# A four-layer image network on one core: the scan rounds of eight images as one sequence, the second layer begun three rounds later, a sigmoid made from tanh

## The chip, the cores and the metric

The kernel runs on one core of one Trainium2 chip, as one launch. The metric is the device time of that launch in microseconds (us), lower is better. The core has five engines that [...] wait for each other through semaphores: PE (matrix products; PEld is its weight load), DVE (element-wise work and scans), ACT (activation functions), POOL (element-wise work; it also issues DMAs) and SP (issues DMAs only). [...]

## What is computed

The input x has 8 images of 384 channels and 32 x 32 pixels, all in float32. Four layers follow each other.

- Layer 0 is a selective state-space scan over the 1024 pixels of an image, forwards and backwards, beside a local branch. For each image the input is normalised over channels, projected to u and z, u is convolved with 4 taps, and from it come a step size delta and the rows B and C (16 states each). Then, for each channel and each of the 16 states,

```python
deltaA = jnp.exp(delta[..., None] * A)
deltaBu = (delta * u)[..., None] * Bm[:, :, None, :]

def step(h, inp):
    dA, dBu, c = inp
    h = dA * h + dBu
    return (h, jnp.einsum('bdn,bn->bd', h, c))
```

  The sum over states, plus u * D, is multiplied by silu(z) and projected out. The local branch is a depthwise 3 x 3 convolution whose sigmoid gates the normalised input; both are added to x with two learned scales.
- Layer 1 is a convolution block, a linear attention over 8 heads and an MLP of 384 to 1536 to 384 with gelu, each with a residual.
- Layers 2 and 3 are depthwise convolutions with large kernels, a pointwise convolution and a gelu. The change does not touch them.

## The kernel before, in words

Layers 0 and 1 are written in `_layers01`, image by image, and the two layers of different images are interleaved by hand. Three Python generators hold the work of one image; each `yield` ends one step and names its cost in units of about one 128x128 by 128x512 product.

- `front(b)` (from L572) is layer 0 ahead of the scan: normalisation (`ms`, L581 to L586), in-projection (`in`, `uz`, L592 to L605), local branch (`lc`, `lg`, `xr`, L608 to L623), 4-tap convolution (`ut`, `uc`, L626 to L646), B and C (`xd`, `bc_d`, L648 to L660), step sizes (`dt`, `sp`, `dl`, L662 to L693). Its steps cost 96 units in all. What DVE has to do after ACT is put off by `defer(1, ...)` to a later round: `local` (L617) for the gate, `deltas` (L680) for the step sizes. Results go to DRAM scratch: `dl_d`, `v_d`, `bc_d`, `ud_d`, `z_d`, `x1_d`.
- `scan(b)` (from L695) is the scan: 12 units (2 directions, 2 halves of 512 pixels, 3 channel groups of 128) of 4 rounds, so 48 rounds an image. The forward direction takes half 0 and then half 1, the backward direction half 1 and then half 0. A round handles 4 of the 16 states of 128 channels, as two tiles of 128 x 1024. For each tile ACT makes `da` with four exponentials a round (L776), DVE makes `du` (L781, in PSUM) and runs two scans into `hs` (L793), POOL multiplies by C (L802), and PE sums over states into `acc` (`sums`, L736). The sums are written two rounds late (the list `late`, L785 and L806), so that PE need not wait for POOL. After the fourth round of a unit `acc` goes out: forwards to `yf_d` (L746), backwards times z to `g_d` (L749, L750). The loads of a unit (`dlt`, `vr`, L728, from `dl_d` and `v_d`) are issued on SP one unit ahead, half of them in round 1 of the unit before (L767) and half in its last round (L811); the rows B and C (`bct`, L714) likewise (L788, L809). Only within an image: unit 0 of an image loads everything when the generator starts (L752, L753).
- `layer1(b)` (from L877) is layer 1: out-projection (`op`, `xx`, L881 to L891, which needs `g_d` and `x1_d`), first convolution (`h`, `dw`, L892 to L909), second (`c`, L910 to L923), attention (`kv`, `q`, `den`, `rzb`, `pj`, L927 to L1032), layer norm (`mu`, `var`, L1034 to L1051) and MLP (`mf`, `hm`, `mo`, L1053 to L1085). Its steps cost 328 units.

Two short generators fill in: `fold()` prepares layer-1 weights beside image 0, `kernels` (called `prepare`) the convolution kernels of layers 2 and 3 beside images 1 to 7.

The order of instructions is set in the loop at L1092: while the rounds of `scan(b)` are written, `front(b+1)` and `layer1(b-1)` are written between them. All their work is one sum `need` (90 + 325 + 12 units in the middle images), spread over 47 rounds; the generator that is least far on goes next:

```python
while work and done < need * (i + 1) / (rounds - 1):
    w = min(work, key=lambda w: w[2] / w[1])
```

When the 48 rounds of an image are written, the remaining sums are flushed (L815), then what is left of the two generators, then all that was put off (L1117 to L1120). Only then does the generator of the next image begin, with its loads. ACT and DVE serve scan and layers alike, in the order written: an `op` result that DVE has to add (L890) stands ahead of the scans of the next round. After image 7, `layer1(7)` runs by itself.

Of the kernel before, what the change touches and what calls it, by code (L numbers as in the profile page):

```python
# [1 line left out]

# [6 lines left out]
FP = mybir.dt.float32  # L9
AF = mybir.ActivationFunctionType  # L10
# [4 lines left out]
P = 128  # L15
# [359 lines left out]
def _layers01(tc, nc, B, xv, x2_d, dram, ident, mean_w, eps5, eps6, one, half, minus1, vec, bns, bnt,  # L375
# [12 lines left out]
    with ExitStack() as ctx:  # L388
# [183 lines left out]
        def front(b):  # L572
# [36 lines left out]
            for h in range(2):  # L609
                for c in range(NC):  # L610
                    xr = t2(f"xr_{b}_{h}_{c}")
                    nc.sync.dma_start(xr, xv[b][:, c, bass.ts(h, HALF)])
                    ps = conv3(xn_d, b % 2, h, c, t3, f"lc_{b}_{h}_{c}")
                    lc = t2(f"lg_{b}_{c}_{h}")
                    nc.scalar.activation(lc, ps, AF.Sigmoid, bias=vec("dw_b0", c))

                    def local(h=h, c=c, lc=lc, xr=xr):  # L617
                        nc.vector.tensor_mul(rows(lc), rows(lc), xn[h][c])
                        nc.vector.scalar_tensor_tensor(xr, lc, rs, xr, ALU.mult, ALU.add)
                        nc.gpsimd.dma_start(x1v[b][:, c, bass.ts(h, HALF)], xr)  # L620

                    defer(1, local)
                    yield 3  # L623
# [68 lines left out]
                    defer(1, deltas)  # L692
                    yield 3  # L693

        def scan(b):  # L695

            units = [
                (d, h, c)
                for d in range(2) for h in ((0, 1) if d == 0 else (1, 0)) for c in range(NC)
            ]  # L700
            late = []
# [2 lines left out]
                return t.rearrange("p (j n) -> p j n", n=HALF)  # L704

            def load_bc(k, r):
                d, h, _ = units[k]
                t = sp.tile([P, 2, HALF], FP, tag="bct", name=f"bct_{b}_{d}_{h}_{r}", bufs=4)
                for o in range(2):
                    src = bass.AP(  # L710
                        bc_d.tensor, bc_d[b, d, o * NST + 4 * r, h * HALF].offset,
                        [[0, 32], [L, 4], [1, HALF]],
                    )
                    nc.sync.dma_start(t[:, o, :], src)  # L714
                return t

            def load(k, i):

                d, h, c = units[k]
# [12 lines left out]
            def sums(k, r, hs, acc, y0, zt):  # L732
                d, h, c = units[k]
                cols = bass.ts(h, HALF)
                for j in range(4):
                    nc.tensor.matmul(  # L736
                        acc[32 * j : 32 * j + 32, :], selt, hs[j // 2][:, bass.ts(j % 2, HALF)],
                        start=(r == 0), stop=(r == NR - 1), skip_group_check=True,
                    )
                if r == 0:  # L740
                    nc.tensor.matmul(acc, ident, y0, start=False, stop=False, skip_group_check=True)
# [13 lines left out]
            for k, (d, h, c) in enumerate(units):  # L755
                cols = bass.ts(h, HALF)
                second = k % (2 * NC) >= NC
                for r in range(NR):
# [11 lines left out]
                    end = HALF - 1 if d == 0 else 0  # L770
                    for i in range(2):
                        dlt, vt = now[i]
                        da = sp.tile([P, 2 * HALF], FP, tag="da", name=f"da_{b}_{k}_{r}_{i}", bufs=N_DA)
# [6 lines left out]
                        du = accp.tile([P, 2 * HALF], FP, tag="du", name=f"du_{b}_{k}_{r}_{i}")  # L780
# [8 lines left out]
                        t = sp.tile([P, 2 * HALF], FP, tag="hs", name=f"hs_{b}_{k}_{r}_{i}", bufs=N_HS)  # L789
                        for j in range(2):  # L790
                            s = bass.ts(j, HALF)
                            k_c = carry[:, c * NR + r, 2 * i + j : 2 * i + j + 1]
                            nc.vector.tensor_tensor_scan(  # L793
                                t[:, s][:, way], da[:, s][:, way], du[:, s][:, way],
                                k_c if second else 0.0, ALU.mult, ALU.add,
                            )
# [79 lines left out]

        def layer1(b):  # L877

            xx = []
            w = wtile(outproj_t, f"wo_{b}")  # L880
            for h in range(2):  # L881
                xh, gh = a6(f"xx_{b}_{h}"), a6(f"g_{b}_{h}")
                nc.sync.dma_start(xh, x1v[b][:, :, bass.ts(h, HALF)])
                nc.sync.dma_start(gh, gv[b][:, :, bass.ts(h, HALF)])
                xx.append(xh)
                for m in range(NC):
                    ps = long_psum(f"op_{b}_{m}_{h}")
                    dense(ps, w, m, gh)
# [1 line left out]
                    nc.vector.scalar_tensor_tensor(o, ps, rsm, o, ALU.mult, ALU.add)  # L890
# [198 lines left out]
            tick()  # L1089
        tick(everything=True)  # L1090
        rounds = 4 * NC * NR
        for b in range(B):  # L1092
            work = []
            if b + 1 < B:
                work.append([front(b + 1), 90, 0])
            if b > 0:
                work.append([layer1(b - 1), 325, 0])
            if b == 0:
                work.append([fold(), 30, 0])
            if b == 1:  # L1100
                work.append([some(prepare, 7), 1, 0])
            elif b > 1:
                work.append([some(prepare, 6), 12, 0])
            need = sum(n for _, n, _ in work)
            done = 0
            for i, _ in enumerate(scan(b)):
                tick()

                while work and done < need * (i + 1) / (rounds - 1):
                    w = min(work, key=lambda w: w[2] / w[1])  # L1110
                    cost = next(w[0], None)
                    if cost is None:
                        work.remove(w)
                        continue
                    w[2] += cost
                    done += cost
# [97 lines left out]
```

## Time and profile before

| what | time |
|---|---|
| median of 3 runs (5799.74 to 5806.63) | 5803.92 us |
| the profiled execution | 5806.88 us |
| its span in the trace | 5805.1 us |
| start and `front(0)`, from 0 | 206 us |
| rounds of image 0 | 206 to 734 |
| rounds of image 1 | 734 to 1286 |
| rounds of image 2 | 1286 to 1859 |
| rounds of image 3 | 1859 to 2451 |
| rounds of image 4 | 2451 to 3019 |
| rounds of image 5 | 3019 to 3585 |
| rounds of image 6 | 3585 to 4160 |
| rounds of image 7 | 4160 to 4645 |
| `layer1(7)` by itself | 4645 to 4800 |
| layers 2 and 3 | 4800 to 5805 |

The rounds of an image are counted here from the start of its first `du` on DVE (L781) to that of the next image. The profile gives the busy time of each engine; a table of stretches gives it for each stretch, with the granted TensorE clock (1.00 is full speed) and the share of time that the 16 DMA engines were busy. "x" is a count of instructions; PE shows each float32 product as two records. A group line gives the busy time of like instructions and the mean of one, and after the second bar how long the engine stood idle ahead of them and what ended that.

### The profile page before, as it was taken

What the parts mean: (1) busy time and instruction counts of PE and PEld (TensorE: products, weight loads), DVE (VectorE), ACT (ScalarE), POOL (GpSimd) and SP (SyncE); (2) the same over time, 40 slices, a digit from 0 to 9 for tenths busy, and PEclk for the clock granted to TensorE, in tenths of its full rate; (3) what the DMA queues carried; (4) which work ended last, traced back from release to release, by engine and by line L of the source; (5) the groups of instructions that cost most, each with busy time, mean ns of one, the idle gap of its engine ahead of it and who ended that gap; (6) DMA issues with size and microseconds to landing.
All of it is one profiled execution on the core that took longest, in us unless ns stands there. A gap on an engine that the chain in (4) does not pass through costs nothing. (4 is left out here: it accounts for less than half of the span.)

```text
span 5805.1 us, 57844 instructions
## 1 busy us (share of the span) xinstructions
PE 4813.5 (83%) x19550; PEld 2091.8 (36%) x19550; DVE 3677.1 (63%) x3775; ACT 3064.5 (53%) x4116; POOL 2892.9 (50%) x1603
## 2 busy tenths in 40 slices
PE   4576579977988799879888997899779869899999
PEld 1121124322332243223322332233223324498498
DVE  0399997968687768776878786878678811011211
ACT  1656546874667557846784687468635613000211
POOL 3277676557554656565656564656466700110133
PEclk7687689988999899989999998899889989999999
DMA  9555476677567756764666467646643541366677
GB/s 299 185 176 178 145 247 194 230 188 216 187 197 202 216 173 193 168 204 134 191 205 189 141 175 186 190 140 176 179 145 120 135 96 45 95 165 158 196 166 150
DMA packets 528255, 1012.16 MB, mean 174 GB/s; under 512 B 60616, under 2 KB 196248, under 8 KB 527960
## 3 DMA queue, kind: packets, MB, share of 16 engines
q1 hardware_dynamic: 387952, 665.99, 38.5%
q0 software_dynamic: 71136, 248.53, 16.6%
q10 hardware_dynamic: 68872, 93.95, 5.1%
q8 instruction: 155, 2.54, 0.2%
q14 instruction: 140, 1.15, 0.1%
HBM read 763.86 MB, written 288.36 MB: 181 GB/s over the span
## 5 line engine op out<-in xcount | busy, mean ns | idle before, releaser
L802 POOL TENSOR_TENSOR hs<-hs,bct 128x1024 f32<-128x1024 f32 x768 | 2378.7, 3098 | 1180.4 <-DVE hs L793 665.8
L776 ACT ACTIVATE da<-dlt,neg_a 128x512 f32<-128x512 f32 x1536 | 1031.7, 714 | 848.8 <-DVE hs L793 756.8
L793 DVE TENSOR_TENSOR_SCAN hs<-da,carry,du 128x512 f32<-128x512 f32 x768 | 947.1, 1268 | 445.8 <-PE acc L736 211.0
L781 DVE TENSOR_TENSOR du<-vr,bct 128x1024 f32<-128x1024 f32 x768 | 1048.3, 1365 | 51.7 <-issue 21.7
L793 DVE TENSOR_TENSOR_SCAN hs<-da,du 128x512 f32<-128x512 f32 x768 | 901.2, 1208 | 153.9 <-ACT da L776 74.0
L736 PE MATMUL acc<-hs,selt 128*32 128x512 f32 x3072 | 736.5, 674 | 293.0 <-POOL hs L802 241.7
L1064 PE MATMUL mo<-hm,w 128*128 128x512 f32 x1152 | 562.5, 628 | 84.4 <-ACT hm L1062 60.8
L502 PE MATMUL mf<-ln,w 128*128 128x512 f32 x1152 | 545.7, 614 | 42.8 <-ACT dl L672 40.4
L736 PEld LDWEIGHTS acc<-hs,selt 128*32 128x32 f32 x3072 | 122.3, 115 | 722.2 <-POOL hs L802 391.6
L1064 PEld LDWEIGHTS mo<-hm,w 128*128 128x128 f32 x1152 | 214.9, 197 | 427.8 <-issue 255.1
L776 ACT ACT_TABLE_LOAD x265 | 340.0, 1283 | 39.2 <-DVE hs L793 26.7
L502 PEld LDWEIGHTS mf<-ln,w 128*128 128x128 f32 x1152 | 215.2, 194 | 358.9 <-issue 285.1
L316 PE MATMUL cv_b<-xt_b,toep 128*64 128x256 f32 x2688 | 304.5, 388 | 14.1 <-DVE xt_b L298 14.1
L316 PE MATMUL cv_a<-xt_a,toep 128*64 128x256 f32 x2688 | 304.6, 388 | 9.2 <-DVE xt_a L298 9.2
L502 PE MATMUL in<-xn,win 128*128 128x512 f32 x576 | 289.1, 633 | 26.0 <-ACT phi_k L874 24.2
L511 PE MATMUL dw<-dw_i,t3b 96*32 96x512 f32 x1152 | 238.0, 707 | 86.4 <-DMA dw_i<-h_d 86.3
L316 PEld LDWEIGHTS cv_b<-xt_b,toep 128*64 128x64 f32 x2688 | 282.5, 199 | 36.6 <-issue 16.2
L316 PEld LDWEIGHTS cv_a<-xt_a,toep 128*64 128x64 f32 x2688 | 282.4, 199 | 31.1 <-issue 10.4
L511 PE MATMUL lc<-lc_i,t 96*32 96x512 f32 x1152 | 218.1, 679 | 57.2 <-issue 28.8
L511 PE MATMUL c<-ut,t 128*32 128x512 f32 x768 | 195.2, 676 | 45.6 <-DMA ut<-u_d 32.1
L502 PE MATMUL op<-g,wo 128*128 128x512 f32 x288 | 143.1, 647 | 86.7 <-DMA g<-g_d 58.7
L1062 ACT ACTIVATE hm<-mf,biasf 128x512 f32<-128x512 f32 x192 | 130.7, 687 | 145.2 <-PE mf L502 143.5
(189 smaller groups left out, 5618.3 us busy)
## 6 DMA issues: line engine op xcount, KB each, us to landing
dlt<-dl_d SPq DMA_DIRECT2D x384, 256.0 KB, 4.5
vr<-v_d SPq DMA_DIRECT2D x384, 256.0 KB, 4.7
bct<-bc_d SPq DMA_DIRECT2D x256, 256.0 KB, 4.1
ut<-u_d SPq DMA_DIRECT2D x192, 257.5 KB, 5.0
lc_i<-xn_d SPq DMA_DIRECT2D x192, 228.8 KB, 4.9
dw_i<-h_d SPq DMA_DIRECT2D x192, 228.8 KB, 4.1
tp_d<-g_d POOLq DMA_DIRECT2D x64, 672.0 KB, 7.2
w<-w_d SPq DMA_DIRECT2D x64, 576.0 KB, 5.8
```

Of the source, the lines that this page charges most:

```text
L316: nc.tensor.matmul(ps[2 * H * e : 2 * H * (e + 1), 0:BW], tp[:, 2 * (g % (GB // 2)) + e, :, :, t].rearrange("p c j -> p (c j)"), rhs, star ...
L502: nc.tensor.matmul(ps, w[:, k, m * P : (m + 1) * P], rhs[k] if isinstance(rhs, list) else rhs[:, k, :], start=(k == 0), stop=(k == NC - 1),)
L511: nc.tensor.matmul(ps[32 * j : 32 * j + 32, :], lhs(j, i), rhs(j, i), start=(i == 0), stop=(i == taps - 1), skip_group_check=True,)
L736: nc.tensor.matmul(acc[32 * j : 32 * j + 32, :], selt, hs[j // 2][:, bass.ts(j % 2, HALF)], start=(r == 0), stop=(r == NR - 1), skip_group ...
L776: nc.scalar.activation(da[:, bass.ts(j, HALF)], dlt[:, bass.ts(j, HALF)], AF.Exp, scale=neg_a[:, g, r : r + 1],)
L781: nc.vector.tensor_mul(pairs(du), pairs(vt), bct[r][:, 0:1, :].to_broadcast([P, 2, HALF]),)
L793: nc.vector.tensor_tensor_scan(t[:, s][:, way], da[:, s][:, way], du[:, s][:, way], k_c if second else 0.0, ALU.mult, ALU.add,)
L802: nc.gpsimd.tensor_mul(pairs(t), pairs(t), bct[r][:, 1:2, :].to_broadcast([P, 2, HALF]))
L1062: nc.scalar.activation(hm, ps, AF.Gelu, bias=biasf[:, NC * i + f, :])
L1064: nc.tensor.matmul(acc[m], wb[:, f, m * P : (m + 1) * P], hm, start=(i == 0 and f == 0), stop=(i == FF // C - 1 and f == NC - 1),)
```

## The change

Four things are done.

1. `scan()` is one generator for all images. Its list of units runs over `b` too, so the loads of an image's first unit are issued in the last rounds of the image before (rounds 45 to 47, counted from 0), and the two rounds of late sums are carried over into rounds 0 and 1 of the next image. The flushes at the end of an image are gone; what is put off is forced once an image, in round 43.
2. Each generator has a share of its own, from a first round to a last one: `front(b+1)` rounds 0 to 43 (90 units over 43 rounds), `layer1(b-1)` rounds 3 to 47 (325 units over 44). Before, 47 rounds were shared by all. `layer1` takes half 1 ahead of half 0 in the out-projection and the first convolution.
3. The sigmoid of the local branch is written as tanh(v/2), and DVE makes (t + 1) * xn times half the scale from it: one multiplication becomes a `scalar_tensor_tensor`, and four small DVE instructions at the start make the halved constants.
4. `tc.issue_after` would queue layer work behind the sums of an earlier round. It takes effect only where more than LAG = 1000000 sums are in the list, and there are 384, so it never does.

```diff
+LAG = 1000000
...
+        dwh = wp.tile([P, NC, 1], FP, tag="dwh", name="dwh")
+        for c in range(NC):
+            nc.vector.tensor_scalar_mul(dwh[:, c, :], vec("dw_b0", c), 0.5)
+        rsh = wp.tile([P, 1], FP, tag="rsh", name="rsh")
+        nc.vector.tensor_scalar_mul(rsh, rs, 0.5)
...
-                    nc.scalar.activation(lc, ps, AF.Sigmoid, bias=vec("dw_b0", c))
+                    nc.scalar.activation(lc, ps, AF.Tanh, bias=dwh[:, c, :], scale=0.5)
...
-                        nc.vector.tensor_mul(rows(lc), rows(lc), xn[h][c])
-                        nc.vector.scalar_tensor_tensor(xr, lc, rs, xr, ALU.mult, ALU.add)
+                        nc.vector.scalar_tensor_tensor(
+                            rows(lc), rows(lc), one, xn[h][c], ALU.add, ALU.mult
+                        )
+                        nc.vector.scalar_tensor_tensor(xr, lc, rsh, xr, ALU.mult, ALU.add)
...
-        def scan(b):
+        def scan():
             units = [
-                (d, h, c)
+                (b, d, h, c) for b in range(B)
                 for d in range(2) for h in ((0, 1) if d == 0 else (1, 0)) for c in range(NC)
             ]
...
-            for h in range(2):
+            for h in (1, 0):
                 xh, gh = a6(f"xx_{b}_{h}"), a6(f"g_{b}_{h}")
...
-            for h in range(2):
+            for h in (1, 0):
                 hh, mid = image6(f"hh_{b}_{h}")
...
         rounds = 4 * NC * NR
+        last = rounds - NR + 1
+        summed = []
+        scans = scan()
         for b in range(B):
             work = []
             if b + 1 < B:
-                work.append([front(b + 1), 90, 0])
+                work.append([front(b + 1), 90, 0, last - 2, 0])
             if b > 0:
-                work.append([layer1(b - 1), 325, 0])
+                work.append([layer1(b - 1), 325, 3, rounds - 1, 0])
...
-            for i, _ in enumerate(scan(b)):
+            for i in range(rounds):
+                next(scans)
                 tick()
-
-                while work and done < need * (i + 1) / (rounds - 1):
-                    w = min(work, key=lambda w: w[2] / w[1])
-                    cost = next(w[0], None)
...
-            for w in work:
-                for _ in w[0]:
-                    tick()
-            tick(everything=True)
+                with tc.issue_after(summed[-1 - LAG]) if len(summed) > LAG else nullcontext():
+                    for w in list(work):
+                        gen, need, lo, hi, done = w
+                        while done < need * (i + 1 - lo) / (hi - lo) or i >= hi:
+                            cost = next(gen, None)
+                            if cost is None:
+                                work.remove(w)
+                                break
+                            done += cost
+                            w[4] = done
+                if i == last - 2:
+                    tick(everything=True)
+        next(scans, None)
+        tick(everything=True)
```

More of the change, by code (lines that the diff above doesn't have):

```diff
@@ L1 @@
-from contextlib import ExitStack
+from contextlib import ExitStack, nullcontext
 import concourse.bass as bass
@@ L706, in load_bc @@
             def load_bc(k, r):
-                d, h, _ = units[k]
+                b, d, h, _ = units[k]
                 t = sp.tile([P, 2, HALF], FP, tag="bct", name=f"bct_{b}_{d}_{h}_{r}", bufs=4)
@@ L717, in load @@
             def load(k, i):
-                d, h, c = units[k]
+                b, d, h, c = units[k]
                 ts = []
@@ L732, in sums @@
             def sums(k, r, hs, acc, y0, zt):
-                d, h, c = units[k]
+                b, d, h, c = units[k]
                 cols = bass.ts(h, HALF)
                 for j in range(4):
-                    nc.tensor.matmul(
+                    ins = nc.tensor.matmul(
                         acc[32 * j : 32 * j + 32, :], selt, hs[j // 2][:, bass.ts(j % 2, HALF)],
@@ L740, in sums @@
                 if r == 0:
-                    nc.tensor.matmul(acc, ident, y0, start=False, stop=False, skip_group_check=True)
+                    ins = nc.tensor.matmul(acc, ident, y0, start=False, stop=False, skip_group_check=True)
+                summed.append(ins.ins)
                 if r < NR - 1:
@@ L754, in scan @@
             acc = y0 = zt = nxt = None
-            for k, (d, h, c) in enumerate(units):
+            for k, (b, d, h, c) in enumerate(units):
                 cols = bass.ts(h, HALF)
@@ L772, in scan @@
                         dlt, vt = now[i]
-                        da = sp.tile([P, 2 * HALF], FP, tag="da", name=f"da_{b}_{k}_{r}_{i}", bufs=N_DA)
+                        da = sp.tile([P, 2 * HALF], FP, tag="da", name=f"da_{k}_{r}_{i}", bufs=N_DA)
                         for j in range(2):
@@ L779, in scan @@
                             )
-                        du = accp.tile([P, 2 * HALF], FP, tag="du", name=f"du_{b}_{k}_{r}_{i}")
+                        du = accp.tile([P, 2 * HALF], FP, tag="du", name=f"du_{k}_{r}_{i}")
                         nc.vector.tensor_mul(
@@ L788, in scan @@
                             bct[NR - 1] = load_bc(k, NR - 1)
[L789 removed]
+                        t = sp.tile([P, 2 * HALF], FP, tag="hs", name=f"hs_{k}_{r}_{i}", bufs=N_HS)
                         for j in range(2):
@@ L877, in layer1 @@
         def layer1(b):
-            xx = []
+            xx = [None, None]
             w = wtile(outproj_t, f"wo_{b}")
-            for h in range(2):
+            for h in (1, 0):
                 xh, gh = a6(f"xx_{b}_{h}"), a6(f"g_{b}_{h}")
@@ L884, in layer1 @@
                 nc.sync.dma_start(gh, gv[b][:, :, bass.ts(h, HALF)])
-                xx.append(xh)
+                xx[h] = xh
                 for m in range(NC):
@@ L1094, in _layers01 @@
             if b + 1 < B:
-                work.append([front(b + 1), 90, 0])
+                work.append([front(b + 1), 90, 0, last - 2, 0])
             if b > 0:
-                work.append([layer1(b - 1), 325, 0])
+                work.append([layer1(b - 1), 325, 3, rounds - 1, 0])
             if b == 0:
-                work.append([fold(), 30, 0])
+                work.append([fold(), 30, 0, rounds - 1, 0])
             if b == 1:
-                work.append([some(prepare, 7), 1, 0])
+                work.append([some(prepare, 7), 1, 0, last, 0])
             elif b > 1:
-                work.append([some(prepare, 6), 12, 0])
-            need = sum(n for _, n, _ in work)
-            done = 0
-            for i, _ in enumerate(scan(b)):
+                work.append([some(prepare, 6), 12, 0, rounds - 1, 0])
+            for i in range(rounds):
+                next(scans)
                 tick()
-                while work and done < need * (i + 1) / (rounds - 1):
-                    w = min(work, key=lambda w: w[2] / w[1])
-                    cost = next(w[0], None)
[L1112 to L1116, printed above, removed]
-            for w in work:
-                for _ in w[0]:
-                    tick()
-            tick(everything=True)
+                with tc.issue_after(summed[-1 - LAG]) if len(summed) > LAG else nullcontext():
[12 more added lines that the diff above has]
+        tick(everything=True)
         for _ in prepare:
```

## The prediction

> **What bounds the kernel now.** The profiled execution took 5806.9 us, 1.8 us more than its span of 5805.1 and 3 us more than the median shown (5803.9); I sum against it and take the 3 us off at the end. I read the engine totals first, to see whether one engine is full.
>
> ```profile
> PE 4813.5 (83%) x19550; PEld 2091.8 (36%) x19550; DVE 3677.1 (63%) x3775; ACT 3064.5 (53%) x4116; POOL 2892.9 (50%) x1603
> ```
>
> None is, and the last 1005 us (layers 2 and 3) are not touched. So I cut an image into stretches: image 4, rounds 0-2, 3-11, 12-23, 24-29, 30-35, 36-41 and 42-47. Columns: length, then busy PE, PEld, DVE, ACT, POOL, granted clock, DMA share, GB/s.
>
> ```profile
> 2451.00:2509.00 58.00, 29.34 (x116) 11.41 (x117) 38.32 (x45) 30.37 (x45) 24.48 (x22) 0.68 0.80 175
> 2509.00:2578.00 69.00, 56.07 (x209) 17.80 (x211) 66.17 (x74) 30.99 (x49) 57.64 (x20) 0.90 0.63 198
> 2578.00:2730.00 152.00, 134.68 (x496) 56.33 (x496) 99.79 (x82) 84.16 (x124) 77.41 (x32) 0.97 0.44 137
> 2730.00:2800.00 70.00, 62.36 (x277) 23.38 (x277) 65.01 (x79) 44.97 (x60) 38.36 (x17) 0.93 0.58 172
> 2800.00:2859.00 59.00, 53.31 (x194) 17.39 (x193) 53.62 (x58) 47.08 (x52) 39.47 (x17) 0.97 0.72 226
> 2859.00:2933.00 74.00, 66.59 (x197) 22.48 (x196) 58.29 (x51) 65.34 (x80) 47.12 (x24) 1.00 0.64 190
> 2933.00:3019.00 86.00, 79.38 (x242) 25.70 (x240) 59.10 (x51) 77.72 (x93) 45.88 (x27) 1.00 0.59 190
> ```
>
> The limit changes: DVE in rounds 3-11 (66 of 69) and 24-29 (65 of 70), PE in 12-23 (135 of 152), PE and ACT together at the end (79 and 78 of 86). Only in rounds 0-2 is nobody busy: DVE 38 and PE 29 of 58. What it waits for there is in the list of waits of 2440 to 2510, and in DVE's timeline.
>
> ```profile
> PE op L502 <- DMA g<-g_d: 18.5, 1, 18.5
> DVE xx L890 <- PE op L502: 17.7, 1, 17.7
> ```
>
> ```profile
> 2470.92 1.22 DVE L793 TENSOR_TENSOR_SCAN hs<-da,du 128x512 f32<-128x512 f32 x1
> 2489.86 0.75 DVE L890 SCALAR_TENSOR_TENSOR xx<-op,rsm,xx 128x512 f32<-128x512 f32 x1 [17.71 <-PE op L502]
> ```
>
> The out-projection of the image just finished is written into round 0, needs the last `g_d`, which is just being stored, and DVE stands still before L890 with the scans of round 1 queued behind it. The same table for 80 us around each of the seven changes of image (20 before, 60 after) sums to:
>
> ```profile
> 1266.00:1346.00 80.00, 39.27 (x145) 14.76 (x144) 57.27 (x63) 49.58 (x71) 38.91 (x29) 0.67 0.89 213
> ...
> 3565.00:3645.00 80.00, 50.14 (x173) 17.07 (x171) 60.38 (x66) 50.23 (x71) 37.93 (x32) 0.74 0.78 195
> ...
> sum 560.00, PE 370.97 PEld 131.68 DVE 427.22 ACT 350.53 POOL 279.32; mean PE 53.00 PEld 18.81 DVE 61.03 ACT 50.08 POOL 39.90
> ```
>
> DVE is idle 560 - 427 = 133 us there, PE 189 us. At 1286 it is not the out-projection: ACT's squares of the next `front` wait 16.7 us for a store of `dl_d`, written just before, to free their buffer.
>
> [...] The trace can't show tanh; it shows the sigmoid being loaded 43 times at 1283 ns[...]. [...]
>
> **The change part by part.**
>
> *Change of image.* The loads of the next image's first unit (8 of `dlt` and `vr`, 8 of `bct`, 256 KB each) move from behind the flush into rounds 45-47, as at any other change of unit; there they cost DVE nothing that shows (L781 waited for `vr` 19 us in 384 rounds). The out-projection begins in round 3, with the half stored six units earlier; the other half follows in round 4. The last `g_d` is stored in round 1, three rounds of about 8 us earlier; its store and load take 4.5 and 10.4 us (medians to landing). The squares of the next `front` come four rounds after the last `dl_d` stores. So all three waits go. What is late next is DVE itself, 96% busy in rounds 3-11; at that share 427 us of work keep 17 us idle. Gain 133 - 17 = **116** (bounds 65, the L890 waits of 100.3 us in the profile less 35.4 at the very end, and 133). PE is idle 56 us more than DVE there; it runs behind DVE into rounds 12-23, so what it catches up returns in part: **19**, a third (0 to 56).
>
> *Denser rounds.* `front` goes from 90/47 = 1.91 to 90/43 = 2.09 units a round, `layer1` from 325/47 = 6.91 to 325/44 = 7.39: 0.65 units a round more in rounds 3-42, bought by 20 fewer in rounds 0-2. A unit is 0.88 us of PE: 482 us of an image less 48 rounds of sums at 2.25 (L736 and L741, 736.5 + 127.3 over 384), over 96 + 328 units. In rounds 3-11 DVE hides it. In rounds 12-42 it is 31 x 0.65 = 20 units, and the last 6 of `front` fall into round 43, less 1.4 of `layer1`: 24.6 units, 21.6 us. Rounds 44-47 get 10.3 fewer, 9.1 us. These stages are 89 to 92% PE and hold DVE- and ACT-bound pieces, so I charge 0.6 of both: +13.0 - 5.5 = 7.5 an image, **45** for images 1-6 (bounds 0 and 6 x 21.6 = 130). Image 7 has no `front`; its PE is 392 of 485 us: nothing.
>
> *Round 43.* Everything put off is forced. DVE then waits for ACT's softplus: L683 waited 106.5 us in 30 waits, 3.5 each. Seven of two waits would be 49; the flush of before had them too, in windows that I emptied above, so I give back **10** (0 to 50). Behind them on DVE are the scans of round 44; POOL's stores and then the loads of round 45 wait for that. PE has MLP work meanwhile.
>
> *End.* `layer1(7)` begins with half 1, stored long ago. PE stood 28 us before `op` (10.8 us of work); half of it now fills the wait: **-5** (0 to -10).
>
> *Tanh.* 43 loads of the sigmoid and as many back to exp, 86 x 1.283 = 110 us of ACT. They lie mostly in rounds 21-32; in 24-29 ACT is busy 45 of 70 and DVE idle only 5; I take 2 us an image for seven: **-14** (0 to -40). The DVE form that replaces L618 (876 ns median) is that of L619 (740)[...]: 0 (±10). Four instructions of under 0.3 us at the start: 0, under `front(0)`. `issue_after` never acts: 0.
>
> Sum: -116 - 19 + 45 + 10 - 5 - 14 = -99. 5806.9 - 99 - 3 = **5705 us**.
>
> **The rivals.**
>
> *PE is the true limit of the whole sequence* (chance 0.22). For it: sums fall several rounds behind DVE in rounds 12-17, PE 135 of 152. Then all 189 us return and density costs nothing, since PE's total is unchanged: 5806.9 - 189 - 19 - 3 = 5596. Against: DVE at 96% right after the change of image.
>
> *The stall only moves* (0.10). DVE halts in round 43 for `deltas`, in round 4 for the half just stored; half of the 116 returns, the 19 doesn't: -58 + 45 + 25 - 19 = -7, 5797. [...] Against: 24 us lie between store and use.
>
> *Density wins: slower* (0.13). PE and ACT are both at 90% in rounds 42-47, so an engine's slack is not to be had: rounds 12-43 pay in full, 6 x 21.6 = 130, image 7 pays 31 x 0.48 x 0.88 = 13, and the lighter last rounds are DVE's (8 us of scans each) and return nothing. The change of image gives only the 65 of L890, round 43 costs 49 and tanh and the end give 5: 5806.9 + 143 + 49 - 65 - 5 - 3 = 5926 at worst, 5865 with half of that loss. It decides once the dense rounds cost over 24 us an image.
>
> [...]
>
> **How the numbers follow.** Forecast 0.55 (5640 to 5780), the rivals 0.22, 0.10, 0.13. About 0.2%, 5792 to 5816, is what a measurement of this kernel can tell from no change. Of "moves" 0.04 is within it, the rest faster: faster 0.83, same 0.04, slower 0.13. The range takes in the first rival and the lower part of the second: 5580 to 5795.
>
> **What would show it.** Right: no DVE wait over 10 us for L890 outside the end; 80 us around a change of image with DVE over 75 us busy; rounds 0-2 in 25 to 30 us; rounds 12-42 longer by 10 to 20 us an image; hardly a table load at L615, and some 40 fewer at L776 than its 265. Wrong: rounds 36-43 over 17 us each, a DVE gap in round 43 over 10 us, or PE idle unchanged, moved elsewhere.

## The result, and the profile after

The changed kernel takes 5975.6 us (median of 4 runs, 5959.7 to 5985.4) where the kernel before takes 5805.2 (4 runs beside them). The ratio is 1.0293, 95% interval [1.0266, 1.0319]: 2.9% slower. The forecast was 5705 us, 1.7% faster, with a range up to 5795. The profiled execution took 5982.4 us, its span 5980.6.

The engine totals of the changed kernel (busy us, share of the span, instructions):

```profile
PE 4887.3 (82%) x19550; PEld 2093.6 (35%) x19550; DVE 3658.6 (61%) x3779; ACT 2921.7 (49%) x4018; POOL 2900.1 (48%) x1603
```

ACT has 143 us less to do (3064.5 before), and of the others PE has 74 us more and none else over 10; so most of the 175 us of span are waits that moved or grew. Image 4 in the same stretches of rounds as before (0-2, 3-11, 12-23, 24-29, 30-35, 36-41, 42-47; length, then busy PE, PEld, DVE, ACT, POOL, granted clock, DMA share, GB/s):

```profile
2527.00:2576.00 49.00, 32.51 (x140) 12.29 (x140) 30.50 (x36) 19.68 (x30) 19.42 (x15) 0.83 0.84 162
2576.00:2646.00 70.00, 62.82 (x208) 19.81 (x206) 67.07 (x77) 28.07 (x44) 57.25 (x18) 0.98 0.53 173
2646.00:2785.00 139.00, 121.42 (x449) 50.83 (x448) 100.24 (x81) 75.84 (x115) 77.25 (x32) 0.95 0.47 145
2785.00:2858.00 73.00, 62.82 (x231) 20.16 (x232) 66.06 (x70) 31.19 (x48) 39.02 (x18) 0.89 0.67 208
2858.00:2935.00 77.00, 65.15 (x289) 21.60 (x288) 54.19 (x66) 54.32 (x64) 39.70 (x16) 0.95 0.54 171
2935.00:3037.00 102.00, 90.61 (x250) 29.48 (x249) 58.38 (x56) 82.83 (x100) 49.03 (x31) 0.93 0.53 167
3037.00:3116.00 79.00, 66.39 (x161) 22.98 (x159) 54.30 (x53) 65.54 (x84) 47.07 (x27) 0.93 0.50 166
```

Rounds 0-2 are 9 us shorter, 12-23 are 13 us shorter, and rounds 30-41 take 179 us where they took 133. Summed over images 1 to 6, cut at the rounds where the difference turns (worked out from the starts of `du` and the records of PE):

| rounds | 0-2 | 3-11 | 12-26 | 27-44 | 45-47 | all |
|---|---|---|---|---|---|---|
| before, us | 332 | 434 | 1069 | 1349 | 243 | 3426 |
| after, us | 252 | 477 | 992 | 1650 | 223 | 3594 |
| PE busy before | 192 | 359 | 979 | 1190 | 216 | 2936 |
| PE busy after | 187 | 375 | 869 | 1381 | 181 | 2992 |

So 168 of the 175 us are in images 1 to 6, and rounds 27 to 44 alone lose 302: PE is busy 191 us longer in them (110 come out of rounds 12 to 26; the products of `pj`, the projection behind the attention, take 26 us there before and 144 after), and the other 111 are stops.

Which stops, the waits of PE say, before and after (us in all, times, longest; these sums, and those of the runs below, take in the rounds of image 0 too, also where an expectation says images 1 to 6):

```profile
PE op L502 <- DMA g<-g_d: 39.8, 4, 18.5
PE c L511 <- DMA ut<-u_d: 31.3, 18, 3.5
```

```profile
PE c L517 <- DMA ut<-u_d: 144.4, 33, 24.0
PE op L508 <- DMA g<-g_d: 46.6, 4, 21.0
```

The wait for `g`, which the change was forecast to remove, is still there (L890 is now L902, L502 is L508). A new one has come: PE stands up to 24 us for the 4-tap convolution's loads, `ut`, 113 us more in all (111 without image 0, 89 of them in rounds 27 to 44). And the 80 us around each of the seven changes of image sum, after, to:

```profile
3698.00:3778.00 80.00, 60.03 (x215) 22.07 (x214) 64.60 (x70) 39.12 (x57) 50.79 (x26) 0.89 0.75 182
...
sum 560.00, PE 427.19 PEld 155.31 DVE 435.09 ACT 304.48 POOL 325.09; mean PE 61.03 PEld 22.19 DVE 62.16 ACT 43.50 POOL 46.44
```

DVE idles 560 - 435 = 125 us there; it was 133. One such stop in image 2, round 45, in PE's timeline:

```profile
1818.71 1.43 PE L517 MATMUL c<-ut,t 128*32 128x512 f32 x3
1844.10 2.59 PE L517 MATMUL c<-ut,t 128*32 128x512 f32 x4 [23.96 <-DMA ut<-u_d]
```

The loads were issued from 1815.5 on, so they took some 28 us. The DMA view of 1814 to 1844 lists what else was issued, with KB and the median time to landing; below it, what the queues did from 1822 to 1840 (packets, MB, share of 16 engines):

```profile
ut<-u_d SPq DMA_DIRECT2D x4, 257.5 KB, 28.5
x_d<-xx POOLq DMA_DIRECT2D x3, 256.0 KB, 21.1
xi<-in_x SPq DMA_DIRECT2D x1, 768.0 KB, 29.0
```

```profile
DMA packets 478, 1.16 MB, mean 64 GB/s; under 512 B 67, under 2 KB 74, under 8 KB 477
## 3 DMA queue, kind: packets, MB, share of 16 engines
q1 hardware_dynamic: 288, 0.53, 54.9%
q0 software_dynamic: 189, 0.62, 52.2%
```

The DMA engines are full at 64 GB/s, where the whole run averages 169. The three `x_d<-xx` are the last stores of the second layer (L1088, L1076 before): 256 KB each, but in rows of 32 floats, 128 bytes, because an image is a strip in the padded array of layers 2 and 3. There is a burst of three for each half of an image. In the kernel before, the burst in the rounds of image 3, round 40 and on, seen from 2345 to 2360, fills the engines alone:

```profile
DMA packets 187, 0.62 MB, mean 42 GB/s; under 512 B 35, under 2 KB 35, under 8 KB 187
## 3 DMA queue, kind: packets, MB, share of 16 engines
q0 software_dynamic: 187, 0.62, 102.0%
```

42 GB/s at 102%. There PE waits for no load, so no wait named it. In the changed kernel PE makes nine stops of 12 us or more before `c` or `op` in the rounds of images 1 to 7, and each starts 0.6 to 24 us after the last store of such a burst was issued (1217, 1345, 1817, 1944, 2532, 3583, 3727, 4195, 4342 us; stops at 1217, 1367, 1820, 1962, 2556, 3586, 3728, 4197, 4353).

Four of the 13 bursts in these rounds have no such stop behind them. Two of the four, at 2995 and 3122 us, store image 3's results. Beside the burst at 2995 four loads of `ut` were issued as well (`after`, 2996 to 3008):

```profile
ut<-u_d SPq DMA_DIRECT2D x4, 257.5 KB, 8.2
x_d<-xx POOLq DMA_DIRECT2D x3, 256.0 KB, 8.1
```

8.2 us in place of 28.5, with stores of the same size in the same 128-byte rows. So the length of the rows is not the whole reason. Image by image, one of these stores took 17 to 22 us to land (mean of its six, before and after), but 6.5 and 8.0 for image 3 and 6.4 for image 7, the fast ones in both kernels. What sets them apart is where their rows begin: the strip of image b begins at float 6 + 38 b of rows of 312 floats, which is byte 24 + 152 b, and counted from the start of the array only images 3 and 7 (bytes 480 and 1088) begin at multiples of 32 bytes. No run moved the strips by themselves.

The length counts for a part: image 7's stores took 6.4 us in 128-byte rows and 3.2 in pieces of 2 KB (run e6 below), against 16.7 for image 6's rows (before). And what runs beside the slow stores is slow packet by packet: a 4 KB packet of those stores took 1.73 us (before, median of 126 from 2344 to 2358), and the packets of `ut` beside the burst at 1817 took 0.50 us each (median of 252 from 1822 to 1840) where they took 0.085 (256 from 2900 to 2914). Why a packet of `ut` takes longer there, no run shows.

### The profile page after: what moved, and what is told of

Read it like the earlier page. It is cut to its first block, busy times and chain, and to the rows that moved or that the text cites. A ratio compares the mean times of both kernels' runs of the same rounds, so it can differ in the third digit from the quotient of the medians.

```text
span 5980.6 us, 57602 instructions
## 1 busy us (share of the span) xinstructions
PE 4887.3 (82%) x19550; PEld 2093.6 (35%) x19550; DVE 3658.6 (61%) x3779; ACT 2921.7 (49%) x4018; POOL 2900.1 (48%) x1603
## 5 line engine op out<-in xcount | busy, mean ns | idle before, releaser
L747 PE MATMUL acc<-hs,selt 128*32 128x512 f32 x3072 | 793.3, 663 | 352.6 <-POOL hs L814 298.8
L793 DVE TENSOR_TENSOR du<-vr,bct 128x1024 f32<-128x1024 f32 x768 | 1017.3, 1325 | 81.5 <-DMA vr<-v_d 62.4
L1076 PE MATMUL mo<-hm,w 128*128 128x512 f32 x1152 | 572.8, 638 | 50.8 <-ACT hm L1074 50.0
L508 PE MATMUL mf<-ln,w 128*128 128x512 f32 x1152 | 550.4, 619 | 12.8 <-ACT dl L680 12.8
L1076 PEld LDWEIGHTS mo<-hm,w 128*128 128x128 f32 x1152 | 218.6, 201 | 408.3 <-issue 240.7
L508 PEld LDWEIGHTS mf<-ln,w 128*128 128x128 f32 x1152 | 219.5, 197 | 328.3 <-issue 292.9
L788 ACT ACT_TABLE_LOAD x229 | 293.8, 1283 | 17.9 <-DMA dlt<-dl_d 10.1
L517 PE MATMUL lc<-lc_i,t 96*32 96x512 f32 x1152 | 232.8, 723 | 77.1 <-DMA lc_i<-xn_d 29.4
L317 PEld LDWEIGHTS cv_a<-xt_a,toep 128*64 128x64 f32 x2688 | 282.5, 199 | 31.0 <-issue 10.4
L508 PE MATMUL in<-xn,win 128*128 128x512 f32 x576 | 284.2, 625 | 1.8 <-ACT phi_k L886 1.5
L508 PE MATMUL op<-g,wo 128*128 128x512 f32 x288 | 148.8, 658 | 101.6 <-DMA g<-g_d 81.7
```

The lines of the kernel that those rows point to most:

```text
L317: nc.tensor.matmul(ps[2 * H * e : 2 * H * (e + 1), 0:BW], tp[:, 2 * (g % (GB // 2)) + e, :, :, t].rearrange("p c j -> p (c j)"), rhs, star ...
L508: nc.tensor.matmul(ps, w[:, k, m * P : (m + 1) * P], rhs[k] if isinstance(rhs, list) else rhs[:, k, :], start=(k == 0), stop=(k == NC - 1),)
L517: nc.tensor.matmul(ps[32 * j : 32 * j + 32, :], lhs(j, i), rhs(j, i), start=(i == 0), stop=(i == taps - 1), skip_group_check=True,)
L747: ins = nc.tensor.matmul(acc[32 * j : 32 * j + 32, :], selt, hs[j // 2][:, bass.ts(j % 2, HALF)], start=(r == 0), stop=(r == NR - 1), skip ...
L788: nc.scalar.activation(da[:, bass.ts(j, HALF)], dlt[:, bass.ts(j, HALF)], AF.Exp, scale=neg_a[:, g, r : r + 1],)
L793: nc.vector.tensor_mul(pairs(du), pairs(vt), bct[r][:, 0:1, :].to_broadcast([P, 2, HALF]),)
```

## The experiments

The runs came from several chips, on which the kernel before took 5761 to 5805 us; so each is compared by its ratio to the kernel before on the same chip. The changed kernel is 1.0293, which on those chips is some 5930 us: the us of the first four expectations, written against 5805, are to be read so. "Flat" means contiguous stores.

| run | edit | ratio to before, 95% |
|---|---|---|
| e1 | changed, sigmoid back | 1.0297 [1.0280, 1.0313] |
| e2 | before, tanh alone | 1.0111 [1.0089, 1.0133] |
| e3 | changed, second layer from round 0 | 1.0293 [1.0270, 1.0316] |
| e4 | changed, one budget | 1.0261 [1.0241, 1.0280] |
| e5 | changed, flat | 0.9987 [0.9977, 0.9996] |
| e6 | before, flat | 0.9824 [0.9804, 0.9844] |
| e7 | changed, front ends at 36 | 1.0011 [1.0004, 1.0018] |
| e8 | changed, stores spaced | 1.0128 [1.0112, 1.0145] |
| e9 | front at 36, flat | 0.9937 [0.9922, 0.9953] |
| e10 | front at 36, spaced | 0.9918 [0.9903, 0.9933] |
| e11 | e10, second layer from round 0 | 1.0132 [1.0113, 1.0151] |
| e12 | before, tanh, flat | 0.9929 [0.9910, 0.9947] |
| e13 | before, Relu ahead of Abs | 0.9987 [0.9974, 1.0001] |
| e14 | before, `vr` ahead of `dlt` | 1.0022 [1.0014, 1.0030] |
| e15 | changed, Relu ahead of Abs | 1.0330 [1.0311, 1.0348] |
| e16 | changed, `vr` ahead of `dlt` | 1.0295 [1.0279, 1.0311] |
| e17 | e10, sigmoid back | 1.0049 [1.0030, 1.0069] |
| e18 | changed, one budget, flat | 0.9946 [0.9928, 0.9964] |

### One part of the change at a time

Theory A was density: the same work squeezed into fewer rounds. Its rivals were B, loads of `ut` held up behind a load of the next `front` on SP's queue, and C, steps of both generators that fall into the same round because each has a share of its own.

The sigmoid back (e1) and the tanh alone (e2):

```diff
-                    nc.scalar.activation(lc, ps, AF.Tanh, bias=dwh[:, c, :], scale=0.5)
+                    nc.scalar.activation(lc, ps, AF.Sigmoid, bias=vec("dw_b0", c))
```

> The changed kernel with one part undone: the local branch takes the sigmoid again, as before. Everything else is as changed. Theory A (the loss is in the order and the density of the work in rounds 27 to 44): the tanh is worth what the forecast gave it, 14 us, so 5980 to 6000 us; the table loads at L788 go back from 229 to some 270. Rival: the tanh is part of the loss, because work of ACT that used to be spread by its table loads now comes in clumps; then this one is faster than the changed kernel, 5930 or less.

> The kernel before with only the sigmoid made from tanh. Theory A: about 14 us less than before, 5780 to 5805 us (5805 would be 0). Rival (the tanh is part of the loss): slower than before by 10 us or more.

e1 equals the changed kernel (1.0297 to 1.0293): neither the 14 us nor the rival's gain. e2 is 1.1% slower than before, as the rival said, although ACT's table loads fall from 265 to 227. So the tanh gains nothing in either place. PE's waits for `ut` are 77 us in e1 for 144, and 88 in e3 below, with no time won: their sum alone doesn't measure the loss.

e3, the earlier start of the second layer:

```diff
-                work.append([layer1(b - 1), 325, 3, rounds - 1, 0])
+                work.append([layer1(b - 1), 325, 0, rounds - 1, 0])
```

> The changed kernel with the second layer begun in round 0 again (its 325 units over 47 rounds, 6.91 a round for 7.39), still half 1 first, all else as changed. Theory A, density: the later start squeezes 0.48 units more into each round of 3 to 46, which is 31 x 0.48 x 0.88 = 13 us of PE work an image in rounds 12 to 42; undoing it gives back up to 7 x 13 = 90 us, less the wait for the last g that returns in round 0 (0 to 60 us): 5890 to 5950 us. Theory B (the loads of ut wait behind a load of the next front on SP's queue, whatever the density) and theory C (the steps of the front and of the second layer fall together because each has a share of its own): no gain, 5960 to 6020 us.

1.0293: no gain. 0.48 units a round less and not a microsecond back: density of the second layer, theory A as I had put it, falls.

e4, one budget with the same starts, ends and total for each round:

```diff
-                    for w in list(work):
-                        gen, need, lo, hi, done = w
-                        while done < need * (i + 1 - lo) / (hi - lo) or i >= hi:
+                    while True:
+                        own = [w for w in work if w[2] <= i]
+                        due = [w for w in own if i >= w[3]]
+                        if not own or not (due or total < want[i]):
+                            break
+                        w = min(due or own, key=lambda w: w[2] + (w[3] - w[2]) * w[4] / w[1])
```

> The changed kernel with the same starts, ends and work for each round, but the steps of the three generators taken from one budget a round, the one that is furthest behind first, as the kernel before took them; the changed kernel lets each generator fill its own share. So the density is that of the change, and only the coincidence of steps (a dt or c1 step with one or two MLP steps in the same round) is less. Theory C (coincidence): most of the 76 us an image is not lost, 5850 us or less. Theories A (density) and B (SP's queue): 5950 to 5990 us.

1.0261: the coincidence of steps is worth 0.3% at most, not the loss. PE still waits 124 us for `ut`.

### The stores

With A and C gone (e3 and e4 don't speak against B), I turned to what ran during the stops, and found the bursts. Theory D: the loads wait behind these stores.

e5 and e6, contiguous stores. The values then land in the wrong places of the padded array, so the flat runs are probes and no kernels to use:

```diff
-                            x2v[
-                                m, :, h * (H // 2) : (h + 1) * (H // 2),
-                                PADW + b * (W + PADW) : PADW + b * (W + PADW) + W,
-                            ],
-                            rows(o),
+                            bass.AP(
+                                x2_d.tensor, x2_d[m * P, 0, 0].offset + (2 * b + h) * HALF,
+                                [[row, P], [1, HALF]],
+                            ),
+                            o,
```

> The changed kernel, but the last stores of the second layer put their 512 elements a partition into one contiguous piece of 2 KB, where they put 16 rows of 128 bytes: the values land in the wrong places of the array that layer 2 reads, so layers 2 and 3 compute on wrong data in the same time; nothing is left out. Theory D, new from the traces: three such stores together keep all DMA engines busy for some 25 us, and in the changed kernel they meet, in rounds 39 to 45, the last loads of ut that PE stands for (144 us in images 1 to 6, 31 before) and in rounds 0 to 4 the loads of g. Then this kernel loses the stops of 15 to 24 us: ratio to the kernel before 0.995 to 1.010 (the changed kernel: 1.029). Rivals (density, coincidence of steps, SP's order): the stops stay, 1.020 to 1.030.

> The kernel before with the same contiguous stores (same wrong places, same work). Theory D: here the stores of the first half lie in rounds 40 to 42 where PE waits for no load, and those of the second half at the change of image, with the 18.5 us wait for g; so it gains less than the changed kernel does: 0.985 to 0.998 of before. If the stores cost the same in both kernels, both gain alike, some 2%, and theory D falls as the cause of the difference.

The same bytes in 2 KB pieces take the changed kernel from 1.0293 to 0.9987, 3.1%, some 176 us. It is idle time that goes: PE's busy time in images 1 to 6 is 2984 us for 2992. Nor do the wrong values save time later: from the last product of the second layer to the end it is 786 us in e5 and e6, 790 and 792 in the two kernels. The waits of PE in e5:

```profile
PE c L517 <- DMA ut<-u_d: 51.3, 26, 6.2
```

The longest stop for `ut` is 6.2 us, and no wait for `g` is among the dozen largest. But the kernel before gains too, 1.8%, more than I had allowed it. The stores of e6 around the change at 2391 us (median to landing), and the sums of the 80 us windows of e6 and e5:

```profile
x_d<-xx POOLq DMA_DIRECT2D x3, 256.0 KB, 4.5
```

```profile
sum 560.00, PE 421.19 PEld 154.87 DVE 507.35 ACT 372.90 POOL 338.01; mean PE 60.17 PEld 22.12 DVE 72.48 ACT 53.27 POOL 48.29
```

```profile
sum 560.00, PE 472.95 PEld 170.23 DVE 489.38 ACT 320.00 POOL 372.74; mean PE 67.56 PEld 24.32 DVE 69.91 ACT 45.71 POOL 53.25
```

4.5 us to landing for 21.1. And DVE's idle time at the change of image falls from 133 to 53 us in the kernel before, with the layers and scans written in the old order. So 80 of the 133 us that I took for a matter of order were the burst of the second half's stores, which lies right there (issued at 2446 to 2453 us; the 18.5 us wait for `g` ends at 2485).

e7 keeps the true stores and moves the front out of their way; e8 moves the stores apart:

```diff
-                work.append([front(b + 1), 90, 0, last - 2, 0])
+                work.append([front(b + 1), 90, 0, 36, 0])
```

```diff
+                        def store(m=m, o=o):
+                            with tc.issue_after(muls[-1]):
...
+                        spaced.append([2 * m, store])
```

> The changed kernel with the front spread over rounds 0 to 36 in place of 43 (2.5 units a round for 2.09), so that its last c1 steps lie in rounds 31 to 34, before the stores of round 37. Theory D: the long stops for ut go, ratio to before 1.00 to 1.015. Density: the front is denser still in rounds 12 to 36, ratio 1.03 to 1.04.

> The changed kernel with the three stores of a half issued two rounds apart, each behind POOL's latest scan product, in place of one after the other; the same bytes in the same pieces. Theory D: a load of ut then waits for one store (about 8 us) and not three: ratio 1.005 to 1.018. Rivals: 1.025 to 1.035, since nothing else is moved.

Both as theory D said: 1.0011 and 1.0128. In e7 the same wait of PE is

```profile
PE c L517 <- DMA ut<-u_d: 20.0, 10, 5.4
```

although `front` is denser there than in the changed kernel. In e8 it is 91 us, one stop of 21 us included: spacing the stores does not free every load.

Of theory B, that SP's queue holds up the loads of `ut`, these runs leave little: e5 issues the same loads in the same written order, and the long stops go.

### What is left without the stores

Flat, the two kernels stand at 0.9987 and 0.9824. The stores explain 3.06 - 1.76 = 1.3 of the 2.9%; 1.6% stay. They show in rounds 27 to 44 again: over images 1 to 6 these take 1565 us in e5 and 1280 in e6. PE is busy 230 us longer there, which in part is work gone from other rounds, and its wait for POOL's products ahead of the sums is 62 us for 3 (29 in e9 below).

> The changed kernel with the front over rounds 0 to 36 and the contiguous stores (values in the wrong places, as in the other contiguous kernels). It says what is left once the stores are out: contiguous stores alone gave 0.9987 of before (changed) and 0.9824 (before), so 1.6% stay. If these 1.6% are PE work that the change moved into rounds 27 to 44, where the second layer's MLP already fills PE and ACT, then moving the front out of the last rounds takes them back and the gain at the change of image shows: 0.970 to 0.983. If density as such costs (front 2.5 units a round for 2.09), it is slower than the changed one with contiguous stores: 1.000 to 1.010.

> The changed kernel with the front over rounds 0 to 36 and the three stores of a half two rounds apart, in their true places. Each alone gave 1.0011 and 1.0128. Theory D: the front at 36 has already taken the loads of ut out of the stores' way, so spacing adds only what the loads of g and the rest wait for: 0.985 to 0.998. If the two are worth the same wait, 1.000.

> As the kernel with the front over 36 rounds and spaced stores, and the second layer begun in round 0 in place of 3 (6.91 units a round for 7.39). In the changed kernel the same edit moved nothing (1.0293 for 1.0293). Density: up to 1% faster than with the start in round 3. Theory D: the loads of g come back towards the stores of the second half, equal or slower by up to 0.5%.

> The kernel before with the tanh and the contiguous stores. Tanh alone was 1.0111 of before. Its trace has the op of the next image waiting 78 us for g in images 1 to 6, 40 before, behind the stores of round 47. Theory D: the tanh itself costs nothing, the shifted order met the stores; so with contiguous stores the tanh is worth 0 to 14 us: 0.979 to 0.984. If the tanh itself or its order costs 1.1%: 0.990 to 0.996.

e9 is 0.9937: taking the front out of the last rounds takes back 0.5 of the 1.6%, less than my idea wanted. The same move is worth 2.8% with the true stores (e7): most of its gain is the meeting with them. e10 is 0.9918, 0.8% faster than the kernel before and 3.6% faster than the changed one: of the kernels here that store into the true places, the fastest. Over images 1 to 6 its rounds 0-2 and 45-47 take 184 and 203 us (332 and 243 before), 27-44 take 1308 (1349), 12-26 take 1196 (1069). e11 fits neither expectation: the start in round 0, worth nothing in e3, costs 2.1% here. e12 says that the tanh's 1.1% isn't the stores' doing: 0.9824 goes to 0.9929.

So each edit had an effect of its own in each surrounding. Was that scatter? The order on each engine is planned when the kernel is compiled, and even two activations exchanged change it: of ACT's planned sequence, 77% stays in e13. Theory E: equal work scatters by 1%.

```diff
-                        nc.scalar.activation(t, ps, AF.Abs, bias=vec("dt_b", c))
                         nc.scalar.activation(dl, ps, AF.Relu, bias=vec("dt_b", c))
+                        nc.scalar.activation(t, ps, AF.Abs, bias=vec("dt_b", c))
```

```diff
-                for src_d, n in ((dl_d, "dlt"), (v_d, "vr")):
+                for src_d, n in ((v_d, "vr"), (dl_d, "dlt")):
```

> The kernel before with two activations of each dt step, Abs and Relu of the same PSUM tile, written in the other order: the same work, the same starts and rates. The planned order of the engines differs from there on (of PE's some 4,700 planned entries 93% keep their place in the sequence, of ACT's 77%). Theory E (the planner orders all engines anew after any edit, and the time of equal work scatters by about 1%): 0.99 to 1.012, off 1 by more than the interval. Rival (orders are equivalent, only the edit's own work counts): 0.998 to 1.002.

> The kernel before with the loads of vr written ahead of those of dlt: the same loads in the other order on SP's queue, nothing else. Theory E: 0.99 to 1.012. Rival: 0.998 to 1.002.

> The changed kernel with Abs and Relu in the other order. Theory E: the 2.9% that it is slower are one draw; 1.005 to 1.035. If the loss is all in the change's structure (stores that meet the loads of ut, work moved into rounds 27 to 44): 1.026 to 1.032.

> The changed kernel with the loads of vr ahead of those of dlt. Theory E: 1.005 to 1.035; structure alone: 1.026 to 1.032. Together: if both edits leave the kernel before between 0.99 and 1.012 and the changed one above 1.015, the change's loss is more than the scatter; if they overlap, it can't be told from a bad draw.

-0.13, +0.22, +0.37, +0.02%: theory E falls. The loss is in the change; going by these four small edits, effects of 1% are no scatter, those of 0.3 or 0.4% can be.

> The fastest true kernel so far (front over 36 rounds, stores spaced, 0.9918 of before) with the sigmoid in place of the tanh. If the tanh has a cost of its own of some 1%, as in the kernel before, this one is at 0.980 to 0.986. If its effect depends on where the front's third part lies, as in the changed kernel, where undoing it moved nothing: 0.990 to 0.996, the 14 us of table loads included.

> The changed kernel with its steps taken from one budget a round and with contiguous stores (values in the wrong places). With the stores out, the changed kernel is at 0.9987 and the kernel before at 0.9824. If the coincidence of steps of the front and of the second layer is what is left, the clump of step sizes in rounds 36 to 38 (19.0 us a round in image 5) goes and the ratio is 0.983 to 0.988. If it is only the 0.3% that it was with the true stores: 0.995 to 0.998.

e17: in the fastest version the sigmoid costs 1.3% (1.0049 for 0.9918), which neither expectation had; the tanh that cost 1.1% in the kernel before gains here. e18: one budget, flat, is 0.9946, 0.4% better than e5. Coincidence is at most a small part of what is left.

## Why the prediction was wrong

Two terms carry the error, and the second is the larger. Over images 1 to 6, rounds 45 to 47 and 0 to 11 became 57 us shorter, where the change of image and PE's idle time were to give 116 and 19; rounds 12 to 44 became 224 us longer, where rounds 12 to 43 were charged 13.0 an image, 78 in all.

*Change of image (-116).* The step that failed is "So all three waits go". It took the waits for `g` and for the next image's squares as a matter of when things are written. Measured: DVE idle in the windows went from 133 to 125 us, a gain of 8. The squares' waits for stores did go (39 us of ACT, none after), but PE's waits for `g` only fell from 59 to 41, and a new one came: the loads of the next image's first unit, moved into rounds 45 to 47, were to cost nothing that shows, and ACT stood 44 us for their `dlt` in the windows (5 in e5). These transfers meet the slow stores, of which three, those of the second half, come at the change of image in both kernels. e6 shows it from the other side: with fast stores and the old order, 80 of the 133 us go. I priced the load of `g` at its median to landing, 10.4 us; the median hid the burst (17.4 us for the load issued at 3723 us).

*Denser rounds (+45).* The sum priced PE's work and left out what the new end of `front` would meet. The step that failed is the charge of 0.6 of PE's added work, with no load on the path. Rounds 12 to 44 grew by 37 us an image against 13.0, and rounds 27 to 44 alone by 302 in six images. Of the 302, 191 us are PE's busy time, most of it from other rounds (PE is busy 150 us less in rounds 0-2, 12-26 and 45-47). Of the stops, 89 us are PE's added wait for `ut`, and 60 its added wait for POOL's products ahead of the sums (2 before, 62 after), while other waits shrank. The last 4-tap steps used to be written in rounds 41 to 43 and are now in 37 to 39, and the stores of the first half are written in round 37. Ending the front at 36, denser still, is 2.8% faster, and starting the second layer earlier, less dense, moves nothing in the changed kernel: in these two edits it is the place that costs and not the density.

*PE idle (-19).* PE's busy time around the change of image rose by 56 us (371 to 427), as hoped, but its idle time in rounds 27 to 44 rose from 159 to 269.

*Round 43 (+10).* DVE's waits for ACT's softplus went from 77.6 us (27) to 150.4 (41), but only 34 us of them lie in rounds 43 and 44, within the bound of 50. The largest part, 52 us, lies in rounds 37 and 38, which the prediction did not price; how much of it lies on the path no run tells.

*End (-5).* From the end of the last scan to the end: 1157 us before, 1158 after. Nothing came of it.

*Tanh (-14).* That the tanh needs no table load of its own was my estimate. Measured: none stands at its line (L621, 48 activations), where the sigmoid had 43 of 1283 ns (L615), and those ahead of the exponentials went from 265 to 229. The time didn't follow: 0 in the changed kernel (e1), +1.1% alone (e2), -1.3% in e10 (e17). I can't say why its sign changes. The DVE form, priced at 0, took 56.5 us in all (L624, 719 to 2861 ns each) for 71.5 (L618, 665 to 4633); what stretches single ones was not shown.

*The rivals.* "Density wins: slower", at 0.13, had the sign, and its own limit, 24 us an image in the dense rounds, was passed: images 1 to 6 lose 28 each. But 5926 was its worst, and its reason, too much work a round, is not the one that the runs show for the part that is explained. Rounds of over 17 us in 36 to 43, named as a sign of error, came: rounds 36-41 of image 4 took 17.0 us each, rounds 36-44 of image 6 19.7.

*Settled and not.* Shown: the meeting with the slow stores makes 1.3 of the 2.9% (e5, e6), and moving either side out of the way brings back 2.8% (e7) or 1.6% (e8). Open: the other 1.6%. The front's late end has 0.5 of it (e9 against e5), the separate shares 0.4 (e18), little above the scatter; these were not tried together with flat stores, and the rest has no run of its own. Open as well: what makes the stores slow. That it is where their rows begin rests on images 3 and 7, and theory B was not tried by itself.

## What to carry to other kernels

Before you forecast what a new order brings, list the transfers that fill the DMA engines at a low rate, and where they lie: a stretch of full DMA share at a quarter of the usual GB/s (here 42 of 174, in the kernel before) is a road block, and work that needs loads should not be moved into it. A wait at a seam of the program may be such a burst and no matter of order (here 80 of DVE's 133 us were); one kernel with those stores made contiguous tells which. Where the places must stay, see first where the rows begin (a store landed in 6 to 8 us in two images, 17 to 22 in six): with 8 floats of padding for 6, and a whole number of 8 floats a row, every piece here would begin at a multiple of 32 bytes, as those of the fast images 3 and 7 do; this is a proposal that no run tried. When an edit moves two streams of work against each other, vary the end of one of them by a few rounds before you judge the idea: here seven rounds were worth 2.8% while the slow stores lay there, and 0.5% without them.

## What the hardware showed that I had not expected

- A 256 KB store in 128-byte rows, in a group of three, took 17 to 22 us to land on the mean in six images and 6 to 8 us in the two whose rows begin at multiples of 32 bytes; in pieces of 2 KB it took 3 to 7 (e5, e6). The slow burst filled all 16 DMA engines at 42 GB/s; loads beside one took 28.5 us where their median is 4.7.
- Fewer table loads need not save time: 89 fewer in all (e2, 776 to 687), 1.1% slower.
- The places of equal work matter: e10 and e11 differ by three rounds in the start of one generator, and by 2.1%.
